# Flamingo-style gated cross-attention block on one core: score operands in one tile, wider transfers, maxima one patch earlier

## The chip, the cores and the metric

The kernel runs on one core of a Trainium2 chip. The metric is the device time of one execution in microseconds (us), as the median of several runs. The core has TensorE (PE in the profile; PEld is its weight loads), VectorE (DVE), ScalarE (ACT), GpSimd (POOL) and SyncE (SP). SP computes nothing here: it issues nearly all transfers, in program order, and it stands still while an issue waits for its data or its buffer.

## The reference

The reference, cut to what matters here. B is 8, D is 512 rows ("channels"), S is 2048 columns. A patch is 128 columns. The second half (the mHC block, with 50 Sinkhorn sweeps) is not touched by the change except through two helper tiles.

```python
xn = layernorm(x)                              # over S, for each of 512 rows
q = Wq @ xn_patch + bq[:, None]                # (256, 128) for each patch
k = Wk @ xn_patch + bk[:, None]
val = Wv @ ctx_patch + bv[:, None]
# 8 heads of 32 rows each
scores = einsum('bhdi,bhdj->bhij', qh, kh) / sqrt(32)
scores = where(mask > 0, scores, -1e9)
attn = softmax(scores, axis=-1)
o = gelu(einsum('bhij,bhdj->bhdi', attn, vh))
x = x + tanh(g_xattn) * (Wo @ o + bo) * mask
x = x + tanh(g_ffn) * mhc(layernorm(x))        # streams mixed by Sinkhorn matrices
```

## The kernel before

The columns are cut into 32 blocks of 512 (four per batch entry) and 128 patches of 128. A block is two stacks of 256 columns; a stack is two patches. The source is written as one long program of small steps and handed to a list scheduler, which sets the static order on each engine by priorities, by its own costs and by the buffers of the pools. The priorities follow the order in which the steps are called: the string `ORDER = "MeoaMgPlsMMvSMpOM"` is walked once for each patch `t`, and each letter calls one step.

The steps that the change touches, by the lines of the kernel before:

- `proj(n)` (from L260) normalises block `n`, splits it into a high and a low half in fp16, and forms q and k: four output groups `m` (0 and 1 are q, 2 and 3 are k), each 12 matmuls (L288 to L290). Each result is evicted twice into the tile `ev`, by ACT (high half, L292) and by DVE (low half, L293), and stored to a DRAM scratch `qd` by SP (L294), in runs of 512 columns, 1 KB.
- `stack(m)` (from L299) reads the scratch back in the form that the scores need: the 32 rows of a head on partitions, the eight heads along the free dimension. The operand of q, `QS`, has three parts (high, low, high) on partitions 0 to 95, and that of k, `KS`, has (high, high, low), so that one matmul over 96 rows adds the three products that matter. That is six transfers (L307), each of 32 partitions by 8 heads by 256 columns, in runs of 512 B, and a small one for the mask (L312). There are `NS = 3` sets of `QS` and `KS`, used in turn.
- `smax(t)` (from L333) forms the scores of patch `t` once (L340), takes the row maxima on DVE (L343 to L346), transposes them on TensorE (L348), copies them to fp16 on ACT (L350), and SP writes them into rows 97 and 98 of `QS` (L353). `expo(t)` (from L614) forms the scores a second time, transposed and with the maxima already subtracted by these two rows (L621), and ACT takes the exponential (L623). Both use the PSUM pool `ps_s`, which has two buffers. `smax` is called for patch `t + AHEAD` in the step of patch `t`, and `AHEAD` is 3.
- `stats(b)` (from L556) prepares batch entry `b`: four rounds of four transposed tiles of x (`xTt`, L576) into matmuls (L564), and then, for `b` over 0, sixteen tiles of x (`xs`, L600) that ACT squares and sums (L603). All these tiles are 128 by 512 fp32, from the pool `xtp` with `BUF_XTP = 4` buffers.
- `mixp` (from L983), which mixes streams on TensorE late in the kernel, takes two more tiles, `QD` and `HD` (L1017 to L1025), from the same pool.
- In the setup, the weights of q and k are scaled and split into `WqkH` and `WqkL` (L431, L432), and the bias arrives as a column in one small transfer on ACT's queue (L385).

Of the kernel before, what the change touches and what calls it, by code (L numbers as in the profile page):

```python
# [33 lines left out]
XPRE_POOL = lambda b: b < 7  # L34
AHEAD = 3
LXP = 1
# [6 lines left out]
BUF_XNP = 2  # L43
BUF_XTP = 4
BUF_CTP = 2
# [53 lines left out]
def gated_xattn_mhc_kernel(  # L99
# [77 lines left out]

    QS = [ctile([99, NH, SB], F16, f"QS{i}") for i in range(NS)]
    KS = [ctile([99, NH, SB], F16, f"KS{i}") for i in range(NS)]

# [79 lines left out]
    def proj(n):  # L260
# [19 lines left out]
        if NORM0:  # L280
            yield
        qd = qdp.tile([2, 4, 2, P, BLK], F16, tag="qd", name="qd")
        qds[n] = qd
        for m in range(4):
            ps = ps_p.tile([P, BLK], F32, tag="p", name="qk")
            ms = slice(m * P, (m + 1) * P)
            for c in range(4):
                T.matmul(ps, WqkH[:, c, ms], hs[c], start=(c == 0), stop=False)  # L288
                T.matmul(ps, WqkH[:, c, ms], ls[c], start=False, stop=False)  # L289
                mm = T.matmul(ps, WqkL[:, c, ms], hs[c], start=False, stop=(c == 3))  # L290
# [3 lines left out]
            defer(D_QD, "qd", lambda m=m, ev=ev: SY.dma_start(qd[m // 2, 0:2, m % 2].rearrange("t p s -> p t s"), ev))  # L294
            if n == LASTN and m == LASTM:
                last.update(pe=mm, act=ae, dve=ve)
            yield

    def stack(m):  # L299

        n, j = divmod(m, NSB)
        i = m % NS
        flush(lambda e: e[2] == "qd")
        qd = qds[n]
        for dst, side, parts in ((QS[i], 0, (0, 1, 0)), (KS[i], 1, (0, 0, 1))):
            for r, t in enumerate(parts):
                sd = SY.dma_start(  # L307
                    dst[32 * r : 32 * r + 32, :, :],
                    qd[side, t, :, :, j * SB : (j + 1) * SB].rearrange("m (h r) s -> r (m h) s", r=DH),
                )  # L310
# [46 lines left out]
    with tc.tile_pool(name="set", bufs=1) as st:  # L357
# [198 lines left out]
    def stats(b):  # L556

        lgs = xsp.tile([P, 512], F32, tag="lgs", name="lgs", bufs=1)
        for q4 in range(5):
            if q4 > 0:  # L560
                flush(lambda e: e[2] == "st")
                lg = ps_t.tile([P, 512], F32, tag="t", name="lgx")
                for g in range(4):
                    T.matmul(lg[32 * g : 32 * g + 32, :], Wm[:, 4 * q4 - 4 + g, :], xts[g], start=True, stop=True)  # L564
                if q4 == 1:
                    V.tensor_copy(lgs, lg)
                else:
                    V.tensor_tensor(lgs, lg, lgs, ALU.add)
            if q4 < 4:
                xts = []  # L570

                def ld(q4=q4, xts=xts):
                    for g in range(4):
                        xt_ = xtp.tile([P, 512], F32, tag="xTt", name="xTt")
                        k = 4 * q4 + g
                        SY.dma_start(xt_, xT[b, k * P : (k + 1) * P, :])  # L576
                        xts.append(xt_)

                defer(D_ST, "st", ld)
                yield 1  # L580
# [10 lines left out]
        yield 1  # L591
        sq = lnp.tile([P, 4, NBLK], F32, tag="sq1", name="sq1")
        loaded = []
        for i in range(9):
            now = loaded
            loaded = []
            for j in (2 * i, 2 * i + 1) if i < 8 else ():
                c, k = divmod(j, NBLK)
                xs = xtp.tile([P, BLK], F32, tag="xTt", name="xs")
                SY.dma_start(xs, x[b, c * P : (c + 1) * P, k * BLK : (k + 1) * BLK])  # L600
                loaded.append((c, k, xs))
            for c, k, xs in now:
                A.activation(xs, xs, AF.Square, bias=nm[:, c : c + 1], accum_out=sq[:, c, k : k + 1])  # L603
            if b > 1 or i % 3 == 2:
                yield 1
# [377 lines left out]
    def mixp(b, n, maps, inp=False):  # L983
# [230 lines left out]
```

## Time and profile before

| | |
|---|---|
| runs | 1701.85, 1693.76, 1705.0 us; median 1701.85 us |
| the profiled execution | 1693.74 us, span 1692.0 us |
| PE, DVE, ACT, POOL busy | 1487.1, 1201.6, 1065.3, 818.6 us |
| granted TensorE clock, mean | 0.959 of full speed |
| DMA | 330.61 MB, 317486 packets, 66.0% of 16 engines for SP's queue |

The profile is of one execution. "Busy" is the time in which an engine had an instruction of its own running; waiting is not in it. The span is the time from the first to the last instruction; the execution's own time is 1.7 us more. The executions differ by some 11 us, and the profiled one is at the fast end of them.

### The profile page before, as it was taken

What the parts mean: (1) busy time and instruction counts of PE and PEld (TensorE: products, weight loads), DVE (VectorE), ACT (ScalarE), POOL (GpSimd) and SP (SyncE); (2) the same over time, 40 slices, a digit from 0 to 9 for tenths busy, and PEclk for the clock granted to TensorE, in tenths of its full rate; (3) what the DMA queues carried; (4) which work ended last, traced back from release to release, by engine and by line L of the source; (5) the groups of instructions that cost most, each with busy time, mean ns of one, the idle gap of its engine ahead of it and who ended that gap; (6) DMA issues with size and microseconds to landing.
All of it is one profiled execution on the core that took longest, in us unless ns stands there. A gap on an engine that the chain in (4) does not pass through costs nothing.

```text
span 1692.0 us, 32528 instructions
## 1 busy us (share of the span) xinstructions
PE 1487.1 (88%) x10453; PEld 880.8 (52%) x10517; DVE 1201.6 (71%) x3552; ACT 1065.3 (63%) x2046; POOL 818.6 (48%) x1158
## 2 busy tenths in 40 slices
PE   4899989999997988988898988888798999778887
PEld 2555546556655655555555554545455556543233
DVE  7634334666776679868777777777788889878872
ACT  3356475667657666686568765686566667555454
POOL 1322233544454465656466654656557655643211
PEclk9899999999999999999999999999999999899999
DMA  6789897787588556876589664876556575334443
GB/s 202 206 234 276 252 257 182 199 242 219 158 240 232 168 173 196 258 228 204 151 237 281 204 176 137 260 230 179 172 164 203 179 206 148 96 107 143 135 157 125
DMA packets 317656, 330.61 MB, mean 195 GB/s; under 512 B 50535, under 2 KB 215719, under 8 KB 317486
## 3 DMA queue, kind: packets, MB, share of 16 engines
q1 hardware_dynamic: 316238, 328.20, 66.0%
q8 instruction: 83, 1.36, 0.4%
q14 instruction: 87, 0.71, 0.1%
q10 hardware_dynamic: 1248, 0.33, 0.1%
HBM read 226.71 MB, written 101.16 MB: 194 GB/s over the span
## 4 chain that ended last, share of the span: by engine, by line
PE 38%; DVE 20%; DMA 14%; ACT 10%; issue 9%; POOL 8%; SPq 1%; another core or an unknown queue 0%; POOLq 0%; ACTq 0%; DVEq 0%
PE vp L330 5%; DMA xs<-in_x_dram 4%; PE qk L288 3%; PE qk L290 3%; PE qk L289 3%; DVE w L976 3%; PE op L693 2%; DMA out_dram<-w 2%; PE lgx L564 2%; PE op L694 2%; PE op L695 2%; PE u L642 2%; PE u L638 2%; PE smax L340 2%; DMA xt<-in_x_dram 2%
## 5 line engine op out<-in xcount | busy, mean ns | idle before, releaser
L330 PE MATMUL vp<-Wv,ct 128*128 128x256 f32 x1024 | 253.0, 398 | 17.5 <-DMA ct<-in_cx_dram 8.7
L330 PEld LDWEIGHTS vp<-Wv,ct 128*128 128x128 f32 x1024 | 198.0, 199 | 54.4 <-DMA ct<-in_cx_dram 9.5
L876 POOL TENSOR_TENSOR W<-E,uv 128x64 f32<-128x64 f32 x343 | 115.6, 340 | 220.4 <-DVE uv L874 86.3
L976 DVE SCALAR_TENSOR_TENSOR w<-x,Et,w 128x512 f32<-128x512 f32 x180 | 182.8, 1017 | 34.0 <-POOL w L974 24.7
L288 PE MATMUL qk<-xh,WqkH 128*128 128x512 f16 x512 | 196.9, 386 | 11.2 <-DVE ev L293 8.6
L277 POOL TENSOR_TENSOR xl<-xn,xh 128x512 f16<-128x512 f32 x126 | 155.3, 1243 | 97.3 <-ACT xh L275 96.0
L289 PE MATMUL qk<-xl,WqkH 128*128 128x512 f16 x512 | 197.3, 386 | 2.9 <-POOL xl L277 2.9
L290 PE MATMUL qk<-xh,WqkL 128*128 128x512 f16 x512 | 197.3, 385 | 0.0
L870 POOL TENSOR_TENSOR W<-E,uv 128x64 f32<-128x64 f32 x308 | 105.3, 345 | 165.6 <-DVE uv L880 70.9
L343 DVE TENSOR_REDUCE smax<-smax 128x8 f32<-128x1024 f32 x128 | 156.2, 1221 | 39.4 <-PE smax L340 32.3
L623 ACT ACTIVATE e<-sT,ebi,esc 128x1024 f32<-128x1024 f32 x128 | 153.6, 1200 | 22.1 <-PE sT L621 21.9
L878 DVE TENSOR_REDUCE sm<-W 128x16 f32<-128x64 f32 x392 | 99.7, 257 | 84.9 <-POOL W L876 80.2
L293 DVE SCALAR_TENSOR_TENSOR ev<-qk,bqs,ev 128x512 f16<-128x512 f32 x128 | 94.3, 738 | 57.5 <-ACT ev L292 56.5
L693 PE MATMUL op<-gh,WoH 128*128 128x512 f32 x256 | 119.3, 468 | 17.5 <-DVE ev L293 9.5
L699 ACT ACTIVATE junk<-xt,nmean 128x512 bf16<-128x512 f32 x128 | 92.0, 719 | 66.9 <-DVE xt L697 30.4
L270 POOL TENSOR_SCALAR xn<-xt,ln_r,nb 128x512 f32<-128x512 f32 x126 | 115.5, 920 | 36.5 <-DVE nb L254 28.2
L292 ACT ACTIVATE ev<-qk,bqs 128x512 f16<-128x512 f32 x128 | 86.8, 679 | 66.8 <-PE qk L290 66.3
L658 POOL TENSOR_TENSOR o<-o,mb 128x1024 f32<-128x1024 f32 x32 | 76.0, 2375 | 100.0 <-ACT o L653 99.3
L872 DVE TENSOR_REDUCE sm<-W 128x16 f32<-128x64 f32 x352 | 74.4, 214 | 58.9 <-POOL W L870 55.4
L974 POOL TENSOR_TENSOR w<-w,pj 128x512 f32<-128x512 f32 x60 | 78.3, 1306 | 75.4 <-ACT w L969 42.9
L340 PE MATMUL smax<-KS,QS 97*128 97x128 f16 x1024 | 86.5, 226 | 31.4 <-ACT mh L350 14.2
L697 DVE TENSOR_TENSOR xt<-op,xt 128x512 f32<-128x512 f32 x128 | 86.9, 679 | 36.6 <-remote 22.6
(289 smaller groups left out, 3503.3 us busy)
## 6 DMA issues: line engine op xcount, KB each, us to landing
xt<-in_x_dram SPq DMA_DIRECT2D x128, 256.0 KB
ct<-in_cx_dram SPq DMA_DIRECT2D x64, 512.0 KB
qd<-ev SPq DMA_DIRECT2D x128, 256.0 KB
xTt<-in_xT_dram SPq DMA_DIRECT2D x128, 256.0 KB
x1s<-xt SPq DMA_DIRECT2D x128, 256.0 KB
xs<-in_x_dram SPq DMA_DIRECT2D x112, 256.0 KB
QS<-qd SPq DMA_DIRECT2D x192, 128.0 KB
KS<-qd SPq DMA_DIRECT2D x192, 128.0 KB
```

What stands on the lines that cost most here:

```text
L270: G.tensor_scalar(xn, xt[c], rstd1[b][:, c : c + 1], nb1[b][:, c : c + 1], ALU.mult, ALU.add)
L277: (V if n == 0 and c > 1 else G).tensor_tensor(l, xn, h, ALU.subtract)
L288: T.matmul(ps, WqkH[:, c, ms], hs[c], start=(c == 0), stop=False)
L289: T.matmul(ps, WqkH[:, c, ms], ls[c], start=False, stop=False)
L290: mm = T.matmul(ps, WqkL[:, c, ms], hs[c], start=False, stop=(c == 3))
L330: T.matmul(ps[:, h, :], ct[:, c, h * P : (h + 1) * P], Wv[:, c, :], start=(c == 0), stop=(c == 3))
L340: T.matmul(sc[:, h, :], q[0:97, h, sl], kk[0:97, h, sl], start=True, stop=True)
L343: V.tensor_reduce(mx, sc, AX.X, ALU.max)
L623: A.activation(e32, sc, AF.Exp, bias=ebi[:, t : t + 1], scale=esc[:, t : t + 1])
L693: T.matmul(ps, WoH[:, e, cs], gh[:, e], start=(e == 0), stop=False)
L876: (G if SK_POOL(b - B + 8) else V).tensor_tensor(W4[:, h], E4[:, h], ub[:, h], ALU.mult)
L976: V.scalar_tensor_tensor(w, x1[j], E[:, n, 4 * j + i : 4 * j + i + 1], w, ALU.mult, ALU.add)
```

## The change

Six edits. First, `QS` and `KS` become the two halves of one tile `QK`. The scratch `qd` is laid out by stack, part, and row within the head, and the columns of the projection weights are permuted to match (rows of one index within the head lie together, over the four heads of a group). So the runs that a stack reads are four heads by 256 columns, 2 KB. Second, with k's parts stored in the order (low, high), the first 64 partitions of both operands are one transfer of 64 partitions, and the last 32 partitions of each are one more: three transfers per stack where there were six. Third, the store of the eviction now has four runs of 512 B per partition where it had two of 1 KB. Fourth, `xTt` and `xs` tiles hold two of the former tiles, with one transfer for the pair; ACT squares a pair in one instruction; the pool has two such buffers (the same bytes). `QD` and `HD` share one pair tile. Fifth, `AHEAD` is 4. Sixth, the setup: permuted writes of `WqkH` and `WqkL`, and four transfers for the bias column.

```diff
-AHEAD = 3
+AHEAD = 4
-BUF_XTP = 4
+BUF_XTP = 2
...
-    QS = [ctile([99, NH, SB], F16, f"QS{i}") for i in range(NS)]
-    KS = [ctile([99, NH, SB], F16, f"KS{i}") for i in range(NS)]
+    QK = [ctile([99, 2, NH, SB], F16, f"QK{i}") for i in range(NS)]
+    QS = [t[:, 0] for t in QK]
+    KS = [t[:, 1] for t in QK]
...
-        qd = qdp.tile([2, 4, 2, P, BLK], F16, tag="qd", name="qd")
+        qd = qdp.tile([2, 2, NSB, 2, P, SB], F16, tag="qd", name="qd")
...
-            ev = evp.tile([P, 2, BLK], F16, tag="ev", name="ev")
-            ae = A.activation(ev[:, 0, :], ps, AF.Identity, bias=bqs[:, m : m + 1])
-            ve = V.scalar_tensor_tensor(ev[:, 1, :], ps, bqs[:, m : m + 1], ev[:, 0, :], ALU.add, ALU.subtract)
-            defer(D_QD, "qd", lambda m=m, ev=ev: SY.dma_start(qd[m // 2, 0:2, m % 2].rearrange("t p s -> p t s"), ev))
+            ev = evp.tile([P, NSB, 2, SB], F16, tag="ev", name="ev")
+            p2 = ps.rearrange("p (j s) -> p j s", j=NSB)
+            hi, lo = (0, 1) if m < 2 else (1, 0)
+            ae = A.activation(ev[:, :, hi, :], p2, AF.Identity, bias=bqs[:, m : m + 1])
+            ve = V.scalar_tensor_tensor(ev[:, :, lo, :], p2, bqs[:, m : m + 1], ev[:, :, hi, :], ALU.add, ALU.subtract)
+            defer(D_QD, "qd", lambda m=m, ev=ev: SY.dma_start(qd[m // 2, m % 2].rearrange("j t p s -> p (j t) s"), ev.rearrange("p j t s -> p (j t) s")))
...
-        for dst, side, parts in ((QS[i], 0, (0, 1, 0)), (KS[i], 1, (0, 0, 1))):
-            for r, t in enumerate(parts):
-                sd = SY.dma_start(
-                    dst[32 * r : 32 * r + 32, :, :],
-                    qd[side, t, :, :, j * SB : (j + 1) * SB].rearrange("m (h r) s -> r (m h) s", r=DH),
-                )
+        SY.dma_start(
+            QK[i][0 : 2 * DH].rearrange("q k (m h) s -> q (k m) (h s)", m=2),
+            qd[:, :, j].rearrange("k m t (r h) s -> (t r) (k m) (h s)", r=DH),
+        )
+        for k in range(2):
+            sd = SY.dma_start(
+                QK[i][2 * DH : 3 * DH, k].rearrange("q (m h) s -> q m (h s)", m=2),
+                qd[k, :, j, k].rearrange("m (r h) s -> r m (h s)", r=DH),
+            )
...
-        A.dma_start(bcol, bqk.rearrange("(m p) -> p m", p=P))
+        for m in range(4):
+            A.dma_start(bcol[:, m : m + 1], bqk[m * P : (m + 1) * P].rearrange("(h r) -> r h", r=DH))
...
-        A.copy(WqkH, wq)
-        V.tensor_tensor(WqkL, wq, WqkH, ALU.subtract)
+        vw, vh, vl = (
+            wq.rearrange("p c (m h r) -> p (c m) h r", h=4, r=DH),
+            WqkH.rearrange("p c (m r h) -> p (c m) h r", h=4, r=DH),
+            WqkL.rearrange("p c (m r h) -> p (c m) h r", h=4, r=DH),
+        )
+        A.copy(vh, vw)
+        V.tensor_tensor(vl, vw, vh, ALU.subtract)
...
-                    for g in range(4):
-                        xt_ = xtp.tile([P, 512], F32, tag="xTt", name="xTt")
-                        k = 4 * q4 + g
-                        SY.dma_start(xt_, xT[b, k * P : (k + 1) * P, :])
+                    for g in range(2):
+                        xt_ = xtp.tile([P, 2, 512], F32, tag="xTt", name="xTt")
+                        k = 4 * q4 + 2 * g
+                        SY.dma_start(xt_, xT[b, k * P : (k + 2) * P, :].rearrange("(g p) d -> p g d", p=P))
...
-            for j in (2 * i, 2 * i + 1) if i < 8 else ():
-                c, k = divmod(j, NBLK)
-                xs = xtp.tile([P, BLK], F32, tag="xTt", name="xs")
-                SY.dma_start(xs, x[b, c * P : (c + 1) * P, k * BLK : (k + 1) * BLK])
-                loaded.append((c, k, xs))
-            for c, k, xs in now:
-                A.activation(xs, xs, AF.Square, bias=nm[:, c : c + 1], accum_out=sq[:, c, k : k + 1])
+            if i < 8:
+                xs = xtp.tile([P, 2, BLK], F32, tag="xTt", name="xs")
+                c, k = divmod(i, 2)
+                SY.dma_start(xs.rearrange("p k s -> p (k s)"), x[b, c * P : (c + 1) * P, 2 * k * BLK : 2 * (k + 1) * BLK])
+            if i > 0:
+                c, k = divmod(i - 1, 2)
+                A.activation(now, now, AF.Square, bias=nm[:, c : c + 1], accum_out=sq[:, c, k : k + 1])
...
-        QD = xtp.tile([P, P, 4], F32, tag="xTt", name="QD")
-        HD = xtp.tile([P, 4, 32, 4], F32, tag="xTt", name="HD")
+        qh = xtp.tile([P, 2, 512], F32, tag="xTt", name="QD")
+        QD = qh[:, 0].rearrange("p (t i) -> p t i", i=4)
+        HD = qh[:, 1].rearrange("p (g t i) -> p g t i", g=4, i=4)
```

More of the change, by code (lines that the diff above doesn't have):

```diff
@@ L563, in stats @@
                 for g in range(4):
-                    T.matmul(lg[32 * g : 32 * g + 32, :], Wm[:, 4 * q4 - 4 + g, :], xts[g], start=True, stop=True)
+                    T.matmul(lg[32 * g : 32 * g + 32, :], Wm[:, 4 * q4 - 4 + g, :], xts[g // 2][:, g % 2], start=True, stop=True)
                 if q4 == 1:
@@ L591, in stats @@
         yield 1
[L592 to L593 removed]
+        sq = lnp.tile([P, 4, 2], F32, tag="sq1", name="sq1")
+        xs = None
         for i in range(9):
[L595 to L603 removed]
+            now = xs
+            if i < 8:
[5 more added lines that the diff above has]
+                A.activation(now, now, AF.Square, bias=nm[:, c : c + 1], accum_out=sq[:, c, k : k + 1])
             if b > 1 or i % 3 == 2:
```

## The prediction

> **What bounds the kernel now.** I read the page's head first, then a table of stages, then what TensorE waits for, then one such wait piece by piece.
>
> ```profile
> span 1692.0 us, 32528 instructions
> PE 1487.1 (88%) x10453; PEld 880.8 (52%) x10517; DVE 1201.6 (71%) x3552; ACT 1065.3 (63%) x2046; POOL 818.6 (48%) x1158
> ```
>
> TensorE is the engine nearest its limit: 205 us of 1692 idle. The next is DVE with 490 us. By stages (columns: PE, PEld, DVE, ACT, POOL busy, granted clock, DMA share, GB/s):
>
> ```profile
> 100.00:500.00 400.00, 380.80 (x3004) 234.41 (x3020) 221.50 (x639) 255.10 (x515) 154.54 (x214) 0.99 0.79 225
> 500.00:1000.00 500.00, 441.36 (x3274) 274.27 (x3297) 384.96 (x1060) 343.67 (x672) 287.35 (x385) 0.96 0.71 210
> 1000.00:1490.00 490.00, 423.26 (x3229) 267.75 (x3249) 395.07 (x1147) 332.29 (x630) 290.19 (x410) 0.93 0.62 179
> 1490.00:1692.00 202.00, 170.04 (x556) 65.52 (x557) 138.19 (x587) 99.75 (x176) 58.51 (x117) 0.98 0.41 133
> ```
>
> From 100 to 1490 us (the attention) TensorE is busy 1245.4 of 1390 us, so 145 us are idle; the last 202 us are the mixing, whose order hardly changes. What ends the idle time before TensorE's instructions (total us, times, longest):
>
> ```profile
> PE gTp L667 <- POOL o L658: 24.2, 10, 6.7
> PE smax L340 <- ACT mh L350: 14.2, 9, 3.8
> ...
> PE smax L340 <- DMA KS<-qd: 8.8, 3, 6.8
> ...
> PE lgx L564 <- DMA xTt<-in_xT_dram: 8.3, 7, 2.9
> ...
> PE sT L621 <- DMA QS<-mh: 6.6, 3, 2.5
> ```
>
> No wait is large. Transfers of the scores end 8.8 (KS), 3.7 (QS) and 6.6 us (maxima); the first two are what the new layout aims at. ACT ends some 40 us directly (14.2 of it the copies of maxima). Another 54 go back to ACT through an engine that itself waited for it: 24.2 for POOL's masked `o` (which waited 99.3 us for ACT's `o`), 12.0 behind it on L671, 18.1 for DVE's eviction (which waited 56.5 us for ACT's). So about 94 of 145 us, two thirds, lead to ACT. One wait for a stack, on SP and on PE:
>
> ```profile
> 523.88 0.41 SPq L294 DMA_DIRECT2D qd<-ev  x1
> ...
> 528.73 1.81 SPq L307 DMA_DIRECT2D KS<-qd  x4
> 530.58 0.45 SPq L233 DMA_DIRECT2D xt<-in_x_dram  x1
> 531.08 0.94 SPq L307 DMA_DIRECT2D KS<-qd  x2
> ```
>
> ```profile
> 529.48 0.38 PE L288 MATMUL qk<-xh,WqkH 128*128 128x512 f16 x1
> 536.67 1.01 PE L340 MATMUL smax<-KS,QS 97*128 97x128 f16 x8 [6.81 <-DMA KS<-qd]
> ```
>
> The last eviction is stored at 523.88; k's reads go out at 528.73 to 532.02 with another load in between; TensorE has nothing to do from 529.9 and the maxima start at 536.67, 4.65 us after the last read was issued. The same path over 31 projections, read from the timeline: from the last projection matmul to the end of the last read's issue 8.3 us in the median (11 of 31 over 10, at most 13.4), to the first maxima matmul of that stack 18.4 us. So this path has room now, but not much.
>
> **The change part by part.** Where I count TensorE's work in the changed program, I count instructions of its static order and price them by their spacing in the timeline (0.216 us for a matmul of 512 columns, 0.06 for one of the scores).
>
> (1) Squares on ACT. Their rows:
>
> ```profile
> L603 ACT ACTIVATE xs<-xs,nmean 128x512 f32<-128x512 f32 x112 | 80.2, 716 | 31.5 <-DMA xs<-in_x_dram 29.2 <-DVE nmean L590 2.2
> ...
> L275 ACT CAST xh<-xn 128x512 f16<-128x512 f32 x128 | 76.9, 614 | 24.2 <-POOL xn L270 19.9 <-PE qk L290 2.9
> ...
> L681 ACT CAST gh<-o 128x1024 fp32r<-128x1024 f32 x32 | 33.2, 1037 | 2.5 <-POOL o L658 2.5
> ...
> L603 ACT ACTIVATION_READ_ACCUMULATOR xs<-xs,nmean 128x1 f32 x112 | 21.1, 189 | 0.0
> ```
>
> Before: 112 x (716 + 188 ns for the readout of the sum, its own instruction) = 101 us. A pair has 1024 columns. The trace has no such square; a copy of 512 takes 614 ns, and L681's copy of 1024 takes 1037, so 512 columns more cost 423. After: 56 x (716 + 423 + 188) = 74 us. ACT is freed of 27 us. It is not the bounding engine, so between 0 and 27 of it shows; I take two thirds, the share of TensorE's idle time that leads to ACT: **-18 us**. A long square also holds ACT 0.42 us longer against an exponential behind it; that is inside the bound at 0.
>
> (2) Issues on SP. 384 reads of stacks at 0.44 us (medians 438 and 442 ns) become 192: -84 us. `xTt` 128 to 64 at 0.38 us: -24. `xs` 112 to 56 at 0.37: -21. Together -130 us of SP's 721 us of issue time, 18%. If the new shapes cost as much as the dearest issue (645 ns, the store of maxima), the reads save 45 instead of 84 and the 128 eviction stores (382 ns) cost 34 more: -56. Queued behind these on SP are loads, stores of `w` and of `x1s`. ACT waits 124.5 us for transfers (44.9 for stores of `w`, 30.8, 29.2, 12.7 and 6.9 for loads and other stores). If that falls with the issues by 18%, 22 us, and two thirds show, it is -15; TensorE's own 20.8 us (8.8 + 3.7 + 8.3 for `xTt`) give another 4. **-19 us**, bounds 0 and -26 (all of the 22 shows).
>
> (3) Bytes are unchanged. From the trace's packet records by size: 98,944 packets of 512 B at 35.3 ns, 66,240 of 1 KB at 49.8, 101,767 of 2 KB at 103.9. The reads of stacks go from 98,304 of 512 B to 24,576 of 2 KB (217 to 160 us of 16 engines' time), the stores from 32,768 of 1 KB to 65,536 of 512 B (102 to 145). Net -15 us of some 1117 busy, and the DMA share in no stage of the table is over 0.8: **0**, with -15 and +15 as bounds. An engine moves 14.5 B/ns in 512 B runs here and 19.7 in 2 KB runs, and the stores give back three quarters of what the reads gain. One rule speaks against the long runs: the Trainium skill, "DMA: Bandwidth & Descriptors", section Specifications, has 512 B as the least transfer at line rate, so by it the reads would gain nothing and the stores lose nothing, and the sum would be the same; the rate of 14.5 against 19.7 does not bear it out.
>
> (4) Maxima four ahead, the good side. Between the transposition of a patch's maxima and its second scores lie 16.5 us of TensorE's work in the median before, 25.7 after. The waits of L621 for the maxima (6.6 for the transfer, 2.8 for ACT's copy) should go: **-9 us**, bounds 0 and -9.
>
> (5) Maxima four ahead, the other side. The first maxima of a stack need it a patch earlier. From the last projection matmul to them the static order has 16.6 us of other work before and 11.8 after; for the reuse of the buffer set it is 25.6 and 14.7, which still covers a stack. Before, 16.6 us of work took 18.4 us of time, so I expect 13.6. The path needs 8.3 + 4.65 = 12.95 in the median: covered by 0.65 us. With the eleven late ones of the 31 (10.1 to 13.4 + 4.65) the excess over 13.6 sums to 27 us; 0.5 fewer issues lie in between (3.7 to 3.1), which takes 2 off; 12.5 are paid today: **+12 us**. Bounds: -12.5 (all such waits vanish) and +80 (31 waits of 3 us, see the rival). What is late behind such a wait is all of TensorE's queue: the second scores, and with them ACT's exponential.
>
> (6) The two buffers of `ps_s`. In the static order, a buffer left by maxima is wanted again within 2.5 us of work 28 times (before 15), one left by an exponential 14 times (before 7). The shortfall to 2.5 us sums to 16.6 us before, and the profile's waits of this kind are 18.7 (14.2 + 4.1 + 0.4), so the count is a fair measure. After, it is 33.9: +17, of which the quarter at first maxima of stacks is already in (5), and 2 less for DVE's maxima: **+11 us**, bounds 0 and +17.
>
> (7) Setup. Three more issues on ACT's queue, where one takes 0.39 us, wait for a transfer each; ACT idles 11.2 us before L241 in the setup, which hides them, or 5 us if it did not. The permuted `WqkH` and `WqkL` (1.9 and 2.3 us) lie on the path to the first projection: **+1**, bounds 0 and +4. The evictions in two pieces have the element counts of L292 and L293: 0. DVE's L646 also works in two pieces, of 256 in 407 ns against 738 for 512; by twice that a piece would cost 76 ns, at most 10 us of DVE in all. The pair buffers hold the bytes of before; a pair is freed only as a whole, and TensorE's 8.3 us for `xTt` bound that.
>
> Sum: -18 - 19 - 9 + 12 + 11 + 1 = **-22 us**: span 1670, execution 1671.7. The profiled execution (1693.74) is 0.48% under the median (1701.85), so the median should be near 1671.7 x 1.0048 = **1680 us**, 1.3% less.
>
> **The rivals.** A, *hidden anyway*. ACT is 67% busy in the attention and SP under half, so their relief may show by a third only: -9 - 10 - 9 + 24 = -4, a median of 1698. For it: TensorE is at 95% up to 500 us, where the DMA is busiest, and DVE at 77 to 81% after that is not relieved at all. Against it: two thirds of the idle time lead to ACT. B, *the stack comes late*. The transfer of 64 partitions has k's and q's parts in one, so it must wait for the last eviction; with k's last part 640 KB must then land where 384 KB did. At the attention's mean of 203 GB/s that is 1.3 us more. If the first maxima wait 3 us in each of 31 blocks, (5) is 93 - 12.5 = +80 and the sum +46: span 1738, median 1748, slower. It decides from a mean wait of 1.5 us, where the gain is gone, and costs over 1% from 2.0 us. For it: the margin of 0.65 us, the waits at 358 and 530 us. Against it: six reads of stacks fewer per block on SP, where today's late issues come from. C, *more than counted*: if SP's and ACT's relief show in full and the stack waits vanish, -27 - 26 - 9 - 12.5 + 12 = -62.5 and a median near 1640. A list scheduler orders everything anew, so each case has some 10 us of its own spread.
>
> **How the numbers follow.** Runs differ by 0.7%, so about 1% is what a measurement can tell from no change. Forecast with C's side (faster by over 1%, under 1685): 0.44. A (1685 to 1719): 0.30. B and lesser forms of it: 0.26. The range reaches from C's end, 1640, to a mean wait of about 2.3 us in B, 1728; the forecast's own range is 1655 to 1700.
>
> **What would show it.** Squares: 56 at about 1.14 us, ACT near 1038 us busy. Packets near 277,000, or 7,000 fewer if pairs of `xs` go in 4 KB; DMA share near 65%. L621 (its line after) waiting for maxima under 2 us. First maxima waiting for stacks 25 us in all; over 45 speaks for B. Waits for ACT's copy of maxima and for exponentials near 30 us. The forecast is wrong if TensorE's idle time from 100 to 1490 us is not under 135 us, and A is right if ACT's work falls by 27 us while that idle time stays.

## The result, and the profile after

The changed kernel takes 1713.7 us in the median of 6 runs (1710.41 to 1716.28), the kernel before beside it 1700.98 us: the ratio is 1.0077, with a 95% interval of 1.0058 to 1.0096. It is slower by 0.8%, where 1680 us were forecast. The head of its page:

```profile
span 1714.5 us, 31901 instructions
...
PE 1488.2 (87%) x10454; PEld 887.6 (52%) x10517; DVE 1201.9 (70%) x3552; ACT 1051.1 (61%) x1930; POOL 823.9 (48%) x1158
```

TensorE is as busy as before (1487.1) and idle for 226 us instead of 205. ACT's work fell, though by 14 us and not by 27. The stages of the attention (columns as before: length, PE, PEld, DVE, ACT, POOL busy, granted clock, DMA share, GB/s):

```profile
100.00:500.00 400.00, 374.27 (x2919) 229.14 (x2935) 207.85 (x592) 244.88 (x460) 147.99 (x196) 0.97 0.76 218
500.00:1000.00 500.00, 446.45 (x3391) 281.19 (x3413) 378.43 (x1078) 337.95 (x625) 287.24 (x396) 0.96 0.73 215
1000.00:1490.00 490.00, 415.88 (x3136) 264.38 (x3155) 401.56 (x1139) 325.88 (x602) 294.01 (x408) 0.93 0.63 180
```

From 100 to 1490 us TensorE is idle for 153 us (before 145; under 135 was the mark of the forecast). The first stage holds fewer matmuls than before, the second more, the third fewer again: something is lost early, regained in the middle, and lost at the end. What ends the idle time before TensorE's instructions (total us, times, longest):

```profile
PE smax L348 <- DMA QK<-qd: 39.3, 16, 4.8
PE op L707 <- DVE ev L297: 19.5, 14, 4.6
PE gTp L681 <- POOL o L672: 16.9, 4, 7.0
...
PE lgx L579 <- DMA xTt<-in_xT_dram: 10.0, 10, 3.2
...
PE sT L635 <- ACT mh L358: 6.9, 6, 2.6
...
PE smax L348 <- ACT mh L358: 2.7, 2, 2.3
```

The waits for stacks went from 12.5 us (8.8 for `KS`, in the prediction; 3.7 for `QS`, in the row below) to 39.3; those for the transfer of maxima (6.6) are gone, and those for ACT's copy at the maxima fell from 14.2 to 2.7:

```profile
PE smax L340 <- DMA QS<-qd: 3.7, 2, 2.6
```

One of the 16 waits for a stack, on SP and then on PE:

```profile
918.39 0.35 SPq L614 DMA_DIRECT2D xs<-in_x_dram  x1
921.15 0.64 SPq L310 DMA_DIRECT2D QK<-qd  x1
921.84 0.59 SPq L315 DMA_DIRECT2D QK<-qd  x1
```

```profile
923.01 0.38 PE L292 MATMUL qk<-xh,WqkL 128*128 128x512 f16 x1
927.90 1.01 PE L348 MATMUL smax<-QK 97*128 97x128 f16 x8 [4.52 <-DMA QK<-qd]
928.71 1.06 PE L635 MATMUL sT<-QK 99*128 99x128 f16 x8
929.56 4.60 PE L338 MATMUL vp<-Wv,ct 128*128 128x256 f32 x12
```

The read of 64 partitions is issued at 921.15, and its stack can be used 6.8 us later. And the wait costs more than its 4.52 us. In the same trace, twelve matmuls of `vp` took 2.75 us at 917.71; here, just behind the wait, twelve take 4.60. The clock column of the stages around it (third from the right) says why:

```profile
922.50:926.50 4.00, 0.71 (x3) 0.10 (x1) 1.30 (x5) 3.98 (x10) 2.74 (x5) 0.98 0.94 218
926.50:933.20 6.70, 5.29 (x25) 4.61 (x26) 3.33 (x12) 6.66 (x9) 1.86 (x3) 0.50 0.94 303
933.20:940.00 6.80, 6.80 (x50) 4.45 (x48) 2.77 (x7) 3.34 (x9) 5.15 (x5) 1.00 1.06 305
```

The granted clock is a half for 6.8 us after the gap. Such stretches of 3.4 us or multiples of it follow most gaps of TensorE of about 2 us and more; the mean clock of the profiled executions fell from 0.959 to 0.946. The Trainium skill, "TensorE: Matmul & The Clock Gate", section "Why this matters for your kernels", advises against gaps of more than about 3 us; here a wait for a stack of 2.2 us was already followed by 3.4 us at half clock.

**Where the time lies.** The profiled execution of before was at the fast end of its runs. For a fair comparison by stages I use the kernel with the common tile alone (told below): it has before's steps in before's order, and its span of 1702.9 us is that of a median run. It and the changed kernel, from the two timelines (blocks are counted from 0, so block 8 is the ninth):

| us | order of before (common tile) | changed | difference |
|---|---|---|---|
| first projection block ends | 43.6 | 51.5 | +7.9 |
| block 8 ends | 361.7 | 377.4 | +15.7 |
| block 16 ends | 705.6 | 716.7 | +11.1 |
| last projection block ends | 1427.5 | 1422.5 | -5.0 |
| last second scores (`sT`) end | 1483.5 | 1485.7 | +2.2 |
| last output matmul (`op`) ends | 1513.9 | 1527.1 | +13.2 |
| end | 1702.9 | 1714.5 | +11.6 |

At each of these points TensorE has done nearly the same work in both kernels. From block 8 to the last projection the changed kernel gains 21 us. That isn't the relief of ACT and SP that was forecast: the kernel with four ahead alone, with neither pairs nor layout, takes 1051 us for this stretch (the changed one 1045, the order of before 1066), and the one with the pairs alone 1070. Of all the kernels below, those with four ahead take 1037 to 1053 us and those with three 1059 to 1087. The gain is lost in three places: 8 us up to the end of the first block, another 8 up to block 8, and 18 in the last 100 us of the attention. The second loss doesn't need the first: the kernel with pairs and four ahead, which has the setup of before, ends its first block at 44.1 us and block 8 at 377.8. The first and the third have rows of their own. The start, the casts of ACT and DVE, before and then changed:

```profile
25.61 1.90 ACT L431 CAST WqkH<-wq 128x2048 f16<-128x2048 f32 x1 [1.04 <-DVE wq L430]
...
27.54 2.29 DVE L432 TENSOR_TENSOR WqkL<-wq,WqkH 128x2048 f16<-128x2048 f32 x1 [0.78 <-ACT WqkH L431]
```

```profile
27.54 4.76 ACT L446 CAST WqkH<-wq 128x2048 f16<-128x2048 f32 x1 [1.04 <-DVE wq L439]
...
32.34 4.71 DVE L447 TENSOR_TENSOR WqkL<-wq,WqkH 128x2048 f16<-128x2048 f32 x1 [3.64 <-ACT WqkH L446]
```

The end of the attention, stages of the changed kernel and of the one with the common tile:

```profile
1420.00:1520.00 100.00, 69.87 (x542) 45.95 (x544) 81.60 (x258) 59.32 (x111) 54.23 (x93) 0.80 0.34 101
```

```profile
1420.00:1520.00 100.00, 80.08 (x638) 52.61 (x642) 83.38 (x295) 62.61 (x122) 51.35 (x98) 0.91 0.41 124
```

and what TensorE does there in the changed kernel:

```profile
1445.57 1.01 PE L348 MATMUL smax<-QK 97*128 97x128 f16 x8 [2.34 <-ACT mh L358]
1446.67 1.01 PE L635 MATMUL sT<-QK 99*128 99x128 f16 x8
1450.75 0.27 PE L356 MATMUL smax<-ident,mq 128*16 128x128 f16 x1 [3.07 <-DVE mq L354]
1453.55 1.97 PE L681 MATMUL gTp<-ident,o 128*128 128x128 f32 x8 [2.52 <-POOL o L672]
```

Three waits stand one behind another, each on a different engine, and from 1445 us the clock is a half for 20.5 us. Just before, from 1437.69 us, stand 14 matmuls of the value projection (`vp`); that they could have filled these gaps is a guess. The pair of experiments with `v` moved earlier tells whether the order of the steps is to blame.

### The profile page after: what moved, and what is told of

Its sections match the earlier page's. It is cut to its first block, busy times and chain, and to the rows that moved or that the text cites. A ratio compares the mean times of both kernels' runs of the same rounds, so it can differ in the third digit from the quotient of the medians.

```text
span 1714.5 us, 31901 instructions
## 1 busy us (share of the span) xinstructions
PE 1488.2 (87%) x10454; PEld 887.6 (52%) x10517; DVE 1201.9 (70%) x3552; ACT 1051.1 (61%) x1930; POOL 823.9 (48%) x1158
## 3 DMA queue, kind: packets, MB, share of 16 engines
q1 hardware_dynamic: 263118, 328.18, 65.2%
## 4 chain that ended last, share of the span: by engine, by line
PE 40%; DMA 21%; DVE 19%; ACT 8%; issue 7%; POOL 4%; SPq 1%; another core or an unknown queue 0%; ACTq 0%; POOLq 0%; DVEq 0%
PE vp L338 6%; DMA QK<-qd 4%; DMA xs<-in_x_dram 3%; DVE w L990 3%; DMA xTt<-in_xT_dram 3%; PE qk L290 3%; PE qk L291 3%; PE qk L292 3%; PE op L707 2%; DMA out_dram<-w 2%; PE smax L348 2%; DMA qd<-ev 2%; PE lgx L579 2%; DVE smax L351 2%; PE op L708 2%
## 5 line engine op out<-in xcount | busy, mean ns | idle before, releaser
L338 PEld LDWEIGHTS vp<-Wv,ct 128*128 128x128 f32 x1024 | 203.0, 203 | 56.6 <-issue 17.9
L278 POOL TENSOR_TENSOR xl<-xn,xh 128x512 f16<-128x512 f32 x126 | 163.0, 1305 | 114.4 <-ACT xh L276 112.9
L990 DVE SCALAR_TENSOR_TENSOR w<-x,Et,w 128x512 f32<-128x512 f32 x180 | 177.5, 987 | 41.1 <-POOL w L988 21.1
L707 PE MATMUL op<-gh,WoH 128*128 128x512 f32 x256 | 118.6, 465 | 34.5 <-DVE ev L297 19.5
L892 DVE TENSOR_REDUCE sm<-W 128x16 f32<-128x64 f32 x392 | 98.3, 255 | 57.9 <-POOL W L890 54.2
L348 PE MATMUL smax<-QK 97*128 97x128 f16 x1024 | 86.4, 228 | 50.0 <-DMA QK<-qd 39.3
L271 POOL TENSOR_SCALAR xn<-xt,ln_r,nb 128x512 f32<-128x512 f32 x126 | 108.1, 861 | 32.9 <-DVE nb L255 27.5
L348 PEld LDWEIGHTS <-QK 97*128 97x128 f16 x1024 | 68.8, 102 | 76.7 <-issue 35.1
```

The lines of the kernel that those rows point to most:

```text
L271: G.tensor_scalar(xn, xt[c], rstd1[b][:, c : c + 1], nb1[b][:, c : c + 1], ALU.mult, ALU.add)
L278: (V if n == 0 and c > 1 else G).tensor_tensor(l, xn, h, ALU.subtract)
L338: T.matmul(ps[:, h, :], ct[:, c, h * P : (h + 1) * P], Wv[:, c, :], start=(c == 0), stop=(c == 3))
L348: T.matmul(sc[:, h, :], q[0:97, h, sl], kk[0:97, h, sl], start=True, stop=True)
L707: T.matmul(ps, WoH[:, e, cs], gh[:, e], start=(e == 0), stop=False)
L990: V.scalar_tensor_tensor(w, x1[j], E[:, n, 4 * j + i : 4 * j + i + 1], w, ALU.mult, ALU.add)
```

## The experiments

Each kernel ran beside the kernel before on its chip; ratios are to that, with their 95% intervals. "Order" is the share of TensorE's steps (the sequence of tiles that it writes, taken from the two timelines and aligned) that stand elsewhere than in the kernel before; the changed kernel itself has 73%. The last column is TensorE's waits for the reads of `qd` in one profiled execution; kernels in the order of before show 4 to 15 us there, so single figures of it say little.

| kernel | ratio | interval | order | waits for stacks, us |
|---|---|---|---|---|
| maxima four ahead alone | 0.9981 | 0.9953 to 1.0009 | 52% | 16.6 |
| pairs alone | 1.0086 | 1.0056 to 1.0117 | 54% | 1.5 |
| layout alone, three reads | 1.0178 | 1.0143 to 1.0214 | 35% | 17.6 |
| changed, three ahead | 1.0208 | 1.0180 to 1.0237 | 43% | 12.6 |
| changed, casts written in a row | 1.0079 | 1.0035 to 1.0122 | 73% | 40.8 |
| layout, four ahead, no pairs | 1.0060 | 1.0038 to 1.0082 | 67% | 35.2 |
| permuted weights alone | 1.0044 | 1.0017 to 1.0072 | 0.2% | 4.3 |
| common tile alone | 1.0012 | 0.9987 to 1.0036 | 0.1% | 5.5 |
| pairs, four ahead | 1.0050 | 1.0030 to 1.0070 | 56% | 5.8 |
| changed, four reads | 1.0004 | 0.9975 to 1.0032 | 60% | 8.3 |
| layout, six reads | 1.0052 | 1.0026 to 1.0077 | 0.3% | 15.0 |
| layout, four reads | 1.0234 | 1.0204 to 1.0265 | 44% | 6.6 |
| changed, six reads | 1.0074 | 1.0044 to 1.0104 | 56% | 13.9 |
| before, v and S exchanged | 1.0148 | 1.0116 to 1.0180 | 31% | 6.3 |
| before, v earlier | 1.0012 | 0.9985 to 1.0038 | 32% | 8.5 |
| changed, v earlier | 0.9954 | 0.9930 to 0.9977 | 65% | 23.2 |
| four reads, early permutation | 1.0020 | 1.0000 to 1.0041 | 64% | 12.6 |
| the same without pairs | 1.0054 | 1.0033 to 1.0076 | 77% | 14.9 |

**The parts one by one.** First the parts were put together and taken apart: the changed kernel with maxima three ahead, the maxima alone, the pairs alone, the layout alone (with its setup).

In the changed kernel:

```diff
-AHEAD = 4
+AHEAD = 3
```

> The changed kernel with AHEAD = 3 and nothing else undone. Theory 1 (the maxima one patch earlier cost more than the rest gains): the waits of the first score matmuls for a stack, 39.3 us after the change, fall to 12.5 us or less, and the time to 1690 +- 8 us, below the kernel before, because squares and SP issues stay cheaper. Theory 2 (the new layout itself is late: the last read of a stack is issued 10.1 us after the last projection matmul where it was 8.3): the waits stay over 25 us and the time at 1708 us or more. Theory 3 (the 12 us lost in the setup and the 20 us lost after the last projection are what counts, the middle gains): 1700 to 1708 us, with the first exponential still near 87 us (68.7 before).

In the kernel before, the reverse:

```diff
-AHEAD = 3
+AHEAD = 4
```

> The kernel before with AHEAD = 4 and nothing else changed. Theory 1: waits for stacks rise from 12.5 to 35 us or more, and the time is 1712 to 1725 us, as long as or longer than the changed kernel. Theory 2: the six-transfer layout is early enough, waits stay under 20 us, and the time is within 5 us of 1701. Theory 3: the setup stays at 68.7 us for the first exponential, the stretch after the last projection grows from 274 us to some 290, the time is 1705 to 1715 us.

In the kernel before, the pairs of `xTt`, `xs` and `QD` with `HD`:

```diff
-BUF_XTP = 4
+BUF_XTP = 2
...
-                xs = xtp.tile([P, BLK], F32, tag="xTt", name="xs")
+                xs = xtp.tile([P, 2, BLK], F32, tag="xTt", name="xs")
...
```

> The kernel before with the pair tiles (x transposed, squared x, QD and HD) alone. ACT's squares should take 74.5 us instead of 101.3, SP loses 120 issues. Theory that relief of ACT and SP shows by two thirds, as the prediction had it: 1701 - 18 - 5 = 1678 us. Rival, hidden anyway: within 5 us of 1701. Rival, pairs are too coarse (a pair is freed only as a whole, TensorE waits longer for x transposed): over 1706 us with waits for xTt over 15 us on TensorE (8.3 before).

In the kernel before, common tile, scratch, stores, three reads and setup:

```diff
...
-        qd = qdp.tile([2, 4, 2, P, BLK], F16, tag="qd", name="qd")
+        qd = qdp.tile([2, 2, NSB, 2, P, SB], F16, tag="qd", name="qd")
...
```

> The kernel before with the new layout alone (one tile for both operands, three transfers per stack, stores in four runs, permuted weights and bias), AHEAD = 3, single tiles for x. The setup should be late as in the changed kernel: first projection ends near 51 us (43.4 before). Theory 1: after that it runs as before or slightly better, waits for stacks under 15 us, 1700 to 1709 us. Theory 2: waits for stacks over 20 us and 1710 us or more.

Measured: 1.0208, 0.9981, 1.0086, 1.0178. The parts don't add up. Four ahead is worth nothing alone and 1.3% beside the rest, although the waits for stacks rise from 12.6 to 39.3 us with it. With the layout alone the time is that of theory 2 (1732 us, over 1710), though the waits for stacks (17.6 us) stay under its 20. With the pairs alone ACT has less work, and TensorE waits more for ACT's `VF` and `mh` (14.2 before, in the prediction). The row of `VF` before, and four rows with the pairs:

```profile
PE vp L330 <- ACT VF L331: 6.1, 4, 2.6
```

```profile
PE op L692 <- DVE ev L293: 18.8, 16, 3.5
PE smax L340 <- ACT mh L350: 17.5, 12, 3.3
PE vp L330 <- ACT VF L331: 16.4, 10, 3.7
PE lgx L564 <- DMA xTt<-in_xT_dram: 16.3, 8, 4.4
```

So less work on ACT goes with more waits for ACT. ACT's load doesn't explain that; where the steps stand is the suspect (54% of them elsewhere). The other rival fits as well, though: both of its marks are met, the time over 1706 us and the waits for `xTt` over 15 (8.3 before). What the pairs cost by being coarse and what by the order isn't told apart here.

**The setup.** The casts of the changed kernel with contiguous writes (and strided reads), and in the kernel before the permuted weights with their four bias transfers alone. In the latter the heads' rows of q and k are mixed, so it computes something else, in the same instructions.

```diff
...
-            WqkH.rearrange("p c (m r h) -> p (c m) h r", h=4, r=DH),
+            WqkH.rearrange("p c (m r h) -> p (c m) r h", h=4, r=DH),
...
```

> The changed kernel with one edit: the two permuted setup writes run in the order of their output, so they write WqkH and WqkL contiguously and read the weights in strides instead. Setup theory (writes of 2 bytes in strides of 8 took 4.76 and 4.71 us where 1.90 and 2.29 were before, and the first projection ends 8 us later): both fall under 2.6 us, the first projection ends near 46 us, and the time falls by 5 to 12 us, to 1702 to 1709 us. Rival (the setup is absorbed later by waits that are there anyway): under 3 us won, 1711 us or more.

> The kernel before with the permuted weights and the four bias transfers alone; the stacks still read the old row order, so the heads' rows are mixed up, at the same amount of work. The static orders of TensorE and ACT are those of before. Setup theory: first projection ends 8 us later than in the kernel before, and the whole is 5 to 12 us longer, 1705 to 1711 us. Rival: within 3 us of 1700, the delay is absorbed.

Measured: 1.0079 and 1.0044. The strided reads take 3.77 us on ACT and 3.68 on DVE, so little was mended; the first block ends at 48.3 instead of 51.5 us, and the total stays. The new setup alone, in the order of before, costs 0.44% or 7.5 us: there the loss lasts to the end. In another order it doesn't: the changed kernel with six reads and the kernel with pairs and four ahead (both told below) have the same order and end their first block at 52.0 and 44.1 us, but block 8 at 377.3 and 377.8.

**The common tile**, with six reads and nothing else of the change:

```diff
-    QS = [ctile([99, NH, SB], F16, f"QS{i}") for i in range(NS)]
+    QK = [ctile([99, 2, NH, SB], F16, f"QK{i}") for i in range(NS)]
...
```

> The kernel before with both score operands in one tile, six transfers as before. Theory that the common tile itself makes waits (one buffer set's halves treated as one): waits of TensorE for stacks over 20 us and 1706 us or more. Theory that the tile is nothing and the transfers' shape is what costs: within 3 us of 1700.

Measured: 1.0012. That q and k share a tile costs nothing that the interval shows (0.9987 to 1.0036).

**Layout and four ahead without the pairs**, with the casts written in a row:

```diff
-BUF_XTP = 2
+BUF_XTP = 4
...
-                xs = xtp.tile([P, 2, BLK], F32, tag="xTt", name="xs")
+                xs = xtp.tile([P, BLK], F32, tag="xTt", name="xs")
...
```

> New layout with AHEAD = 4 and the contiguous setup writes, single tiles for x as before: the changed kernel without its pairs and without its slow setup. If the parts add (layout alone +33, pairs alone +15, AHEAD = 4 beside the layout -21, setup -8): 1713.7 - 15 - 8 = 1691 us, below the kernel before. If they do not add (each order of the whole program has its own waits, and pairs hurt only the old order): 1705 us or more.

Measured: 1.0060, beside 1.0079 with the pairs. What costs 0.9% alone makes no difference here that the intervals show.

**Is it the merged read?** First the missing cell, the pairs with four ahead in the kernel before:

```diff
-AHEAD = 3
-BUF_XTP = 4
+AHEAD = 4
+BUF_XTP = 2
...
```

> Before, with the pair tiles and AHEAD = 4, and without the new layout of the score operands. Pairs alone gave 1.0086 and AHEAD = 4 alone 0.9981. If the edits' costs add up: 0.9981 x 1.0086 = 1.007, 1713 us. If AHEAD = 4 takes away what the pairs make late, as it took 21 us off the layout with pairs (1.0208 to 1.0077): about 0.996, 1695 us, with TensorE's waits for ACT's VF (16.4 us with pairs alone) under 8. If pairs and AHEAD = 4 are what is slow in the changed kernel and its layout is innocent: 1.0077 as the changed kernel.

Then the 64 partitions in one read for q and one for k, in the changed kernel:

```diff
-        SY.dma_start(
-            QK[i][0 : 2 * DH].rearrange("q k (m h) s -> q (k m) (h s)", m=2),
-            qd[:, :, j].rearrange("k m t (r h) s -> (t r) (k m) (h s)", r=DH),
-        )
         for k in range(2):
+            SY.dma_start(
+                QK[i][0 : 2 * DH, k].rearrange("q (m h) s -> q m (h s)", m=2),
+                qd[k, :, j].rearrange("m t (r h) s -> (t r) m (h s)", r=DH),
+            )
```

> The changed kernel with its 64-partition read in two, one for q and one for k, q's first: four transfers per stack instead of three. Theory 'the merged read is late' (it must wait for the last eviction, and q's half then lands with k's): TensorE's waits for the stack fall from 39.3 us to under 18, the half-clock stretches behind them with them, and the median from 1713.7 to about 1700 (ratio 1.000). Theory 'the merge is innocent' (the wait is the path from the last matmul over the last store to k's own read, which is as long): waits 30 to 45 us, ratio 1.006 to 1.010. If 32 more issues of 0.54 us on SP weigh: 1.010 and more.

And the layout alone (three ahead, single tiles) with six reads, and with the four above:

```diff
...
+        for k, parts in enumerate(((0, 1, 0), (0, 1, 1))):
+            for r, t in enumerate(parts):
+                sd = SY.dma_start(
+                    QK[i][32 * r : 32 * r + 32, k].rearrange("q (m h) s -> q m (h s)", m=2),
+                    qd[k, :, j, t].rearrange("m (r h) s -> r m (h s)", r=DH),
+                )
...
```

> Before with the new layout (AHEAD = 3, single x tiles), but six reads of 32 partitions per stack as before, in runs of 2 KB. The layout with three reads gave 1.0178. Theory 'the merged read costs': what is left is setup (1.0044) and the common tile (1.0012), so 1.005 to 1.008, about 1712 us. Theory 'the stores of 512 B runs and the changed order cost, however the stack is read': 1.015 to 1.02, about 1730 us.

> The same with four reads per stack (q 64 and 32 partitions, then k 64 and 32). Theory 'the merged read costs': 1.005 to 1.008 as with six, since only the merge of q with k waits for the last eviction. Theory 'stores and order': 1.015 to 1.02. If it is the number of partitions of one read that costs, not the merge of q with k: near the 1.0178 of three reads while six reads give 1.006.

Measured: 1.0050, 1.0004, 1.0052, 1.0234. The changed kernel with four reads does what the theory of the merged read wanted, down to the wait:

```profile
PE smax L348 <- DMA QK<-qd: 8.3, 4, 3.4
```

Three ahead refutes it as the whole cause: there four reads are slower than three (1.0234, 1.0178), though their waits for stacks are shorter (6.6, 17.6 us); POOL's `o`, DVE's `ev`, ACT's `mh` and `VF` take their place:

```profile
PE gTp L682 <- POOL o L673: 32.8, 11, 6.8
PE op L708 <- DVE ev L297: 19.9, 14, 3.7
PE smax L348 <- ACT mh L358: 18.0, 10, 5.4
PE vp L338 <- ACT VF L339: 17.8, 9, 5.9
```

The column of orders sorts these kernels. With as many reads as before the scheduler makes the order of before to within 0.3%, and then the whole layout (512 B stores, 2 KB reads, common tile, setup) costs 0.52%, which is the setup's 0.44% and little else that the intervals show. With three or four reads it makes another order, a third to nearly half of the steps elsewhere, and the time rises by 1.3 and 1.8% more.

**Order alone.** The six reads just shown, in the changed kernel, which gives the order of pairs with four ahead to within 0.1%:

> The changed kernel with six reads of 32 partitions per stack, in runs of 2 KB. Its static order on TensorE after the setup is that of pairs with AHEAD = 4 (1.005), as six reads beside AHEAD = 3 had the order of before (1.0052). Theory 'at a fixed order the layout costs its setup and no more': 1.005 x 1.005 = 1.010, 1718 us, and the merged reads of the changed kernel (1.0077) cost nothing net. Theory 'the merged read is late': below the changed kernel, 1.000 to 1.004.

And the kernel before with two letters of its order string exchanged:

```diff
-ORDER = "MeoaMgPlsMMvSMpOM"
+ORDER = "MeoaMgPlsMMSvMpOM"
```

> Before with two letters of the order string exchanged (v and S: values before statistics), the same work, sizes and transfers; 30% of TensorE's steps stand elsewhere in the static order. Theory 'much of what the edits show is the order that the scheduler draws, and before has a good one': 1.004 to 1.015. Theory 'the order alone is worth nothing, the edits' own costs decide': 0.997 to 1.003.

Measured: 1.0074 and 1.0148. The first repeats the result at a second fixed order: the layout costs 0.24% there (1.0074 to 1.0050, the intervals overlap). And from six reads to the three of the changed kernel, which change the order again, the time stays (1.0074 and 1.0077) while the waits for stacks rise from 13.9 to 39.3 us. The second has before's work on every engine and is 25 us slower. Its main waits were 24.2 and 6.1 us before:

```profile
PE gTp L667 <- POOL o L658: 33.2, 9, 8.1
PE vp L330 <- ACT VF L331: 26.9, 8, 6.6
```

One more order, the same in both kernels:

```diff
-ORDER = "MeoaMgPlsMMvSMpOM"
+ORDER = "MeoaMgPvlsMMSMpOM"
```

> Before with the letter v three places earlier in the order string (before l, s and two M): the same work, 33% of TensorE's steps elsewhere. Theory 'before has a good draw of the order': 1.005 to 1.02, as the first exchange gave 1.0148. Theory 'the first exchange was an unlucky one': 0.997 to 1.003.

> The changed kernel with the same move of v: the same work, 29% of its steps elsewhere. Theory 'the change costs 0.8% in any order': its ratio is 0.8% above that of before with this move. Theory 'the order decides, the edits' own gains and losses nearly cancel': anywhere from 0.995 to 1.02 and within 0.5% of, or below, before with this move; the wait for POOL's o and ACT's VF, not the stack, is what differs.

Measured: 1.0012 for before and 0.9954 for the changed kernel. So the first exchange of letters was an unlucky draw, and this move costs the kernel before nothing. With it the changed kernel is faster, by 0.6% than the kernel before with the same move and by 0.46% than the kernel before; its ratio is the lowest of all (1690.8 us). Its table of milestones is that of the changed kernel up to the last projection (first block 51.6, block 8 376.0, last 1422.4 us), and then it goes another way: the second scores end at 1467.2 instead of 1485.7 and the last output matmul at 1503.5 instead of 1527.1. The end of its attention:

```profile
1420.00:1520.00 100.00, 81.28 (x612) 50.88 (x604) 83.11 (x312) 64.87 (x124) 54.12 (x105) 0.90 0.40 125
```

and its waits for stacks:

```profile
PE smax L348 <- DMA QK<-qd: 23.2, 11, 4.6
```

From 1440 to 1460 us its TensorE is busy for 19.37 of 20 us, where the changed kernel shows 10.22:

```profile
1440.00:1460.00 20.00, 19.37 (x176) 12.85 (x176) 18.61 (x55) 12.69 (x28) 9.94 (x19) 1.00 0.37 117
```

```profile
1440.00:1460.00 20.00, 10.22 (x78) 6.66 (x76) 16.53 (x36) 13.92 (x22) 13.21 (x15) 0.63 0.60 161
```

The work and the transfers are the same in both, so the 18 us at the end are the order's, not the layout's. The expectation was wrong on what would differ: the waits for stacks did, by 16 us, and those for `o` and `VF` were longer (18.6 and 6.7 us; 16.9 and 1.7 in the changed kernel). Nearly all of these 16 us lie before the last projection, which ends at the same time in both, so they weren't what cost.

**Can more be had?** Four reads with the weights permuted early, in ACT's idle time, with the pairs and then without them:

```diff
...
+        wp = stile([P, 4, 512], F32, "wp")
+        A.copy(wp.rearrange("p c (m r h) -> p (c m) r h", h=4, r=DH), wq.rearrange("p c (m h r) -> p (c m) r h", h=4, r=DH))
...
-        wab = stile([P, 4, 512], F32, "wab")
+        wab = wq
...
-        A.copy(vh, vw)
+        A.copy(WqkH, wp)
...
```

> The changed kernel with four reads per stack, and the weights permuted early: ACT writes a permuted fp32 copy while it has nothing else to do, so that the two casts before the first projection are contiguous again (1.9 and 2.3 us instead of 4.76 and 4.71). TensorE's order is that of the four reads but for 6.5%. Theory 'the setup's loss lasts': the first projection block ends at 45 to 48 us (52.6 with four reads), and the ratio is 0.996 (1.0004 less 0.44%). Theory 'a later wait takes it up': 1.000.

> The same without the pair tiles (single xTt and xs, 112 squares). If the pairs cost 0.9% here as alone: 0.988 to 0.992, faster than before. If the four reads and AHEAD = 4 gain only beside them, or the new order is a bad one: 1.000 to 1.010.

Measured: 1.0020 and 1.0054, in both cases near the second theory and without the gain hoped for. The first block ends at 49.7 us and not at 45 to 48: the absolute values of the weights are now written over `wq`, so DVE must wait for the copy, and TensorE's first matmul in the setup waits for DVE until 19.5 us (10.4 in the changed kernel). Without pairs the kernel is slower, not faster.

## Why the prediction was wrong, point by point

The sum of -22 us put 10 us of spread on "a list scheduler orders everything anew" and let it decide nothing. That is the step that failed. At equal work another order gave +1.5% and +0.1% on before and -1.2% on the changed kernel (1.0077 to 0.9954), 25 and 21 us, each as large as the whole forecast. The change moves 73% of TensorE's steps, and the terms were valued as if the kernel kept the order for which the waits had been read. Kernels that share an order lie closer together: 1, 1.0012, 1.0044 and 1.0052 in that of before, 1.0050 and 1.0074 in that of pairs with four ahead, 1.0077 and 1.0079 in that of the changed kernel.

The way to the result can be put together from three of these runs. Pairs and four ahead give 1.0050, the layout with six reads at the same order 1.0074, and three reads instead of six, in a new order, 1.0077. So most of the loss is there without the new layout; how much of this first step is the order's and how much the pairs' own, no run tells.

(1) Squares: the row is as forecast (56 at 1.14 us), but the relief was 16 us and not 27. The durations overlap:

```profile
132.41 1.15 ACT L617 ACTIVATE xs<-xs,nmean 128x1024 f32<-128x1024 f32 x1 [0.61 <-DVE nmean L605]
133.46 0.19 ACT L617 ACTIVATION_READ_ACCUMULATOR xs<-xs,nmean 128x1 f32 x1
133.55 1.13 ACT L617 ACTIVATE xs<-xs,nmean 128x1024 f32<-128x1024 f32 x1
```

The readout starts 94 ns before the square ends, and the next square 94 ns before the readout ends, so a square occupies ACT for 1.14 us with its readout, and for 0.71 before (start to start, medians): 112 x 0.71 - 56 x 1.14 = 16. Two thirds of that, 11 us, would be the term, and the kernel with the pairs alone, 0.86% slower, shows none of it.

(2) SP: the new reads cost more to issue than the 0.44 us taken over from the old ones (medians 636 ns for 64 partitions, 540 for 32). They take 112 us where 168 were spent: 56 saved, not 84. ACT's waits for transfers fell from 124.5 to 109.0 us, 15.5 of the 22 that were forecast. But TensorE's own, 20.8 us that were to fall by 4, rose to 49.3 (39.3 for stacks and 10.0 for `xTt`). What of ACT's 15.5 us shows in the time, no run tells.

(3) The bytes: right. At before's order, 2 KB reads and 512 B stores cost 0.08% beside the setup (1.0052 to 1.0044), within the intervals. The price per packet didn't carry over, though: in the changed kernel, where the 512 B runs are stores, they move 18.1 B/ns and those of 2 KB 18.6, so the net -15 us of DMA time aren't there (66.0% of 1692.0 us before, 65.2% of 1714.5 after, 1117 and 1118 us).

(4) The maxima: the 6.6 us for their transfer are gone, as forecast; the 2.8 for ACT's copy became 6.9. Of the -9 us, 2.5 are left.

(5) The stacks: +12 forecast, +27 measured (39.3 to 12.5), with half clocks behind many of them. In the order with v earlier it is +11 at the same reads. The mechanism was right; its size goes with the order. Rival B named the merged read, but its mark of 45 us was not reached. Four reads brought the waits back to 8.3 us and the time to that of before; at three ahead the same split made the kernel slower, so how much of the 0.8% is the merged read's own can't be told from these runs.

(6) The two score buffers: +11 forecast, and the waits of these kinds fell from 18.7 to 5.6 us (2.7, 0.8 and 2.1). The shortfall counted in the static order was no measure of waits in another order.

(7) The setup: +1 with a bound of +4; 7.5 us in the order of before. I took the element count as the price of a permuted cast, and it costs 2.5 and 2.1 times as much, 5.3 us in all; the casts also start 1.9 us later (27.54 and 25.61).

The 21 us that the changed kernel gains from block 8 to the last projection have the size of the forecast sum, but that is luck. Four ahead alone gains about 15 of them, and in (4) to (6) the prediction had four ahead at -9 + 12 + 11 = +14 us; over the whole kernel, four ahead alone costs nothing (0.9981). The pairs, priced as a gain, gain nothing in that stretch alone. Of the losses, the 18 us at the end of the attention go away when one letter of the order string is moved.

What stays open: why the scheduler's orders differ by so much in time (it plans with costs of its own, which no run here shows), what sets the gain of four ahead in the middle, whether the pairs cost anything at a fixed order, and the price of the merged read at a fixed order; no pair of these kernels with and without it has the same order.

## What to carry to other kernels

Where a list scheduler sets the order, an edit that changes the number of instructions can draw a new order, and here the draw was worth as much as the edits (of two other orders of the kernel before, one cost 1.5% and one nothing): before reading a per cent as the edit's own, compare the orders, measure the spread with an order string that changes nothing else, and hold the order fixed where it can be (here six reads instead of three did that). Then compare by milestones along the span and not by totals of waits, for a gain of 20 us and a loss of 20 us can stand in one run. And price ACT's instructions by the distance from one start to the next, not by their durations.

## What the runs showed of the hardware

- In the changed kernel most gaps of TensorE of 2 to 5 us are followed by 3.4 or 6.8 us at half clock, and several in a row by 20.5 us (from 1445 us). Behind such a gap twelve `vp` matmuls take 4.60 us instead of 2.75. The mean clock doesn't order the kernels, though: the slow order of before (span 1722.2 us) has a mean of 0.954, the fastest kernel 0.955.
- A cast from fp32 to fp16 of 128 x 2048 takes 1.90 us on ACT in a row, 3.77 with strided reads and 4.76 with strided writes of two bytes; DVE's subtraction takes 2.29, 3.68 and 4.71 us.
- SP needs (medians) 636 ns to issue a transfer of 64 partitions with 2 KB runs, 540 ns for 32 partitions, and 440 ns for 32 partitions with 512 B runs: fewer and larger transfers cost more each.
- On ACT the readout of an accumulated sum (188 ns) overlaps the instructions on both sides by 94 ns each.
